# Opening the layers' memory in three steps, with the first projections inside the attention stage, and the attention stage's norm steps moved behind the penalties

## The chip, the cores and the metric

The kernel runs on one core of a Trainium2 chip. A core has five engines that work side by side, each through its own queue in order: TensorE (PE in the profile, with its weight loads as PEld), VectorE (DVE), ScalarE (ACT), GpSimd (POOL) and SyncE (SP), which here issues DMAs. SBUF is the memory that all of them share, PSUM the one that TensorE writes. The metric is device time in microseconds; the median of three runs is given, with the lowest and the highest.

## The reference

Input `x` has 4 batches of 512 tokens of 128 features, all in f32. Two blocks with a residual each:

```python
x = x + attn(layernorm(x))          # 16 heads of 64, 512 x 512 scores, scale 1/8
                                    # penalty -50 above the diagonal, softmax, @ Wr
x = x + layers(layernorm(x))        # 6 layers
```

A layer of the second block is:

```python
x = attn_layer(shift_tokens(x)) + x   # qkv; q, k: l2norm over a head, scales, rotary with xpos;
                                      # softmax over windows of 32 and the window before; @ Wo
x = ffn_layer(shift_tokens(x)) + x    # layernorm * g + b; 128 -> 2 x 341; a * gelu(gate); 341 -> 128
```

`shift_tokens` delays the second half of the features by one token. `layernorm` takes mean and variance over the 128 features.

## The kernel before

Activations are kept transposed, features on the 128 partitions, 512 tokens of a batch along the free axis. The kernel has two stages, and in each the order of the instructions on every engine is the order in which the program writes them (`manual_schedule`). A tile framework adds the waits.

**First stage (lines 132 to 397).** A loop of 64 iterations `m`, each on two blocks of 128 query rows of one pair of heads, plus a 65th that only finishes. Batch `b`, pair of heads `c` and the half `odd` come from `m`: 16 iterations make a batch. An iteration writes, in this order: `times_v1` of work two pairs back, the scores (line 216), the penalties as matmuls on the same banks (229), the first row block's maximum on DVE (241), a v projection (`make_v`, odd iterations, not in the last batch), the transposes of the previous iteration's probabilities (270, copied out by ScalarE at 274 and DVE at 276), the exponentials on ScalarE (247), the next q or k projection (180, 186), the inverse of the sums (256, DVE) and the normalisation on GpSimd (259). A norm's three steps are spread over even iterations and come at the end of each: `mean` (lines 91 to 97: two matmuls with a constant matrix, a subtraction on DVE, a square on ScalarE), `var` (102 to 105: eight small matmuls, then `rsqrt`) and `scale` (110 to 114: four transposes that spread the factor, one product on DVE). `rsqrt` (73 to 85) is a bit trick on DVE and three Newton steps of four instructions each, on the engine that is handed in. `norm_x` of the next batch stands at c = 1, 2, 3 and `norm_x1`, the norm ahead of the second stage, of the batch before at c = 4, 5, 6. `project_out1` (302, 303) closes a batch: 16 matmuls with `wr` and the residual. One PSUM bank, `pj`, serves all projections and norms here; the scores have two pairs of banks, the transposes two banks, `times_v1` one.

**The passage (lines 393 to 400, then 428 on).** After the loop come the last three halves of `times_v1`, then `project_out1` of the last batch. Then the pools of the first stage (`s1`, `ps1`) are closed, and those of the second (`s2`, `ps2`) are opened in the same memory.

**Second stage (from line 400).** 6 layers x 4 batches x 4 blocks of 128 tokens are 96 units. A `slot(n, ...)` handles four units at once, each at another point of its way: unit n+2 (`new`) is projected, rotated and normed; unit n+1 (`nxt`) has its q and k transposed; unit n (`u`) has its scores, softmax and product with v; unit n-1 (`prev`) is projected out. `begin` makes the shifted input (`shift_into`, GpSimd, 416 to 418) and the layer's tables (`layer_tables`, a small DMA at 423 and a product on GpSimd at 425). A unit's way through `new`: `do_project` three times (442), `square` (453, ScalarE), `sum_squares` (458, DVE), `rotate` (463, 467, DVE), `add_rotated` (478, GpSimd), `inverse_norms` (482 and the two seeds on DVE, Newton on GpSimd), `over_norm` (486, GpSimd), `v_windows` (two copies on ScalarE at 520, then 14 to 16 DMAs on SP's queue, 528 to 532). Projections, scores and products with v share three double banks by turns (`two_t`), transposes and the rest two single banks (`one_t`). The first two slots, n = -2 and -1, have no `u`: they fill the pipeline. The last batch's `norm_x1` is called `late`; its three steps stand ahead of slots -2, -1 and 0.

```python
for n in range(-2, len(units) + NT + 3):
    if -2 <= n < 1:
        late[n + 2]()
```

## Time and profile before

| | us |
|---|---|
| median of 3 runs | 2316.82 (2313.41 to 2319.04) |
| the profiled execution, its own time | 2314.14 |
| its span, first to last instruction | 2312.4 |
| start of the first score matmul | 27.17 |
| last transposes of the loop done | 578.7 |
| first scores of the second stage (line 565) | 620.68 |
| scores of the second unit | 638.42 |

The page cuts the span into 40 slices of 57.8 us. Each digit is the busy share of a slice in tenths; the row PEclk is the clock that TensorE was granted.

```
PE   6999999999799999999999999999999999999997
DVE  3665656656678788878877888877888788878773
POOL 1443444444577777766767766767776767766760
PEclk9999999999999999999999999999999999999998
```

The dip in the eleventh slice is the passage between the stages. In the table of instructions in order of time, a row has its start, its duration, engine, line and operation, what it writes and reads, and in brackets how long its engine had been idle and what it waited for. The table of stretches gives for each stretch its length, the busy time of every engine with the number of its instructions, the granted clock, and the share and rate of the DMA engines.

### The profile page before, as it was taken

Reading aid. Unit: us, or ns where it says so; the run is one execution under the profiler, and the core shown is the slowest. Engines: PE = TensorE matmul, PEld = TensorE weight load, DVE = VectorE, ACT = ScalarE, POOL = GpSimd, SP = SyncE. Lnnn points to the kernel's source line nnn. Section 1 sums busy time; section 2 is a strip of 40 time slices with the busy share of each in tenths; the row PEclk is TensorE's granted clock in tenths of the full one; section 3 lists DMA queues with packets and bytes.
Section 4 is the critical chain, followed back from the end, with each engine's and each line's share of the span. In section 5 each row is a group of like instructions: output and inputs, shape, how many; then the busy total and the mean of one; then the engine's idle time right before and its main releaser. Section 6 shows DMA issues by size and latency. Waiting matters only on the chain.

```text
span 2312.4 us, 81596 instructions
## 1 busy us (share of the span) xinstructions
PE 2201.3 (95%) x35088; PEld 1447.7 (63%) x35088; DVE 1710.5 (74%) x2692; ACT 1301.7 (56%) x2166; POOL 1436.1 (62%) x1897
## 2 busy tenths in 40 slices
PE   6999999999799999999999999999999999999997
PEld 3555555555366666666666666666666666666664
DVE  3665656656678788878877888877888788878773
ACT  2554544445255666666666666666566666566662
POOL 1443444444577777766767766767776767766760
PEclk9999999999999999999999999999999999999998
DMA  3000000000222233222322223223332223322220
GB/s 113 1 1 1 1 1 1 1 1 1 46 69 68 63 90 75 62 69 65 90 71 65 71 66 90 68 63 73 73 89 62 71 62 86 80 62 72 66 56 15
DMA packets 91025, 125.81 MB, mean 54 GB/s; under 512 B 25262, under 2 KB 39468, under 8 KB 90668
## 3 DMA queue, kind: packets, MB, share of 16 engines
q1 hardware_dynamic: 90236, 119.02, 21.0%
q8 instruction: 279, 4.57, 0.9%
q10 hardware_dynamic: 432, 1.57, 0.2%
q14 instruction: 78, 0.64, 0.1%
HBM read 20.41 MB, written 1.05 MB: 9 GB/s over the span
## 4 chain that ended last, share of the span: by engine, by line
PE 81%; DVE 14%; ACT 2%; issue 2%; POOL 1%; DMA 1%; SPq 0%; POOLq 0%; ACTq 0%
PE ps_proj L442 19%; PE ps_one L538 13%; PE ps_one L633 7%; PE ps_att L608 6%; PE ps_att L576 6%; PE ps_sc L216 5%; PE ps_o L287 5%; PE ps_pt L270 3%; PE ps_proj L666 3%; PE ps_proj L667 3%; PE ps_proj L680 2%; DVE yt L79 2%; PE ps_sc L229 2%; DVE t L467 2%; DVE rot L463 2%
## 5 line engine op out<-in xcount | busy, mean ns | idle before, releaser
L478 POOL TENSOR_TENSOR rot<-rot,t 128x1024 f32<-128x1024 f32 x192 | 453.9, 2364 | 193.9 <-DVE t L467 188.6
L442 PE MATMUL ps_proj<-wqkv,xs 128*128 128x512 f32 x1152 | 557.5, 607 | 15.3 <-DVE t L467 5.4
L259 POOL TENSOR_TENSOR pr<-pr,den 128x1024 f32<-128x1024 f32 x128 | 240.9, 1893 | 335.3 <-DVE den L256 333.1
L453 ACT ACTIVATE sq<-ps_proj 128x1024 f32<-128x1024 f32 x192 | 196.9, 1025 | 365.9 <-PE ps_proj L442 329.3
L486 POOL TENSOR_TENSOR rot<-rot,ss 128x1024 f32<-128x1024 f32 x192 | 365.4, 1903 | 15.0
L442 PEld LDWEIGHTS ps_proj<-wqkv,xs 128*128 128x128 f32 x1152 | 200.0, 192 | 179.6 <-issue 156.6
L458 DVE TENSOR_REDUCE ss<-sq 128x16 f32<-128x1024 f32 x192 | 233.1, 1214 | 51.4 <-ACT sq L453 50.7
L241 DVE TENSOR_REDUCE nm<-ps_sc 128x2 f32<-128x1024 f32 x128 | 156.0, 1218 | 118.7 <-PE ps_sc L229 118.7
L463 DVE TENSOR_TENSOR rot<-ps_proj,lt 128x1024 f32<-128x1024 f32 x192 | 233.4, 1216 | 0.0
L467 DVE TENSOR_TENSOR t<-ps_proj,lt 128x1024 f32<-128x1024 f32 x192 | 232.8, 1213 | 0.0
L274 ACT COPY pT<-ps_pt 128x512 f32<-128x512 f32 x128 | 75.2, 588 | 264.6 <-PE ps_pt L270 262.9
L633 PEld LDWEIGHTS ps_one<-aT,wo 128*128 128x128 f32 x1536 | 186.3, 192 | 45.3 <-issue 44.5
L538 PE MATMUL ps_one<-ident,rot 128*128 128x128 f32 x1536 | 210.2, 280 | 2.9 <-issue 1.5
L586 DVE TENSOR_REDUCE mx<-ps_att 128x16 f32<-128x1024 f32 x96 | 117.5, 1224 | 97.1 <-PE ps_att L576 95.3
L633 PE MATMUL ps_one<-aT,wo 128*128 128x128 f32 x1536 | 187.3, 275 | 0.4 <-ACT aT L541 0.4
L247 ACT ACTIVATE pr<-ps_sc,nm 128x512 f32<-128x512 f32 x256 | 175.0, 694 | 16.3 <-DVE nm L241 16.3
L82 POOL TENSOR_TENSOR yt<-y 128x32 f32<-128x32 f32 x288 | 68.9, 239 | 181.8 <-DVE y L80 166.6
L538 PEld LDWEIGHTS ps_one<-ident,rot 128*128 128x128 f32 x1536 | 164.4, 141 | 22.1 <-issue 4.6
L608 PEld LDWEIGHTS ps_att<-vw,pT 64*32 64x32 f32 x9216 | 104.0, 106 | 95.5 <-ACT pT L541 54.0
L270 PEld LDWEIGHTS ps_pt<-ident,pr 128*128 128x128 f32 x1024 | 120.0, 142 | 55.9 <-issue 45.8
L608 PE MATMUL ps_att<-vw,pT 64*32 64x65 f32 x9216 | 129.6, 226 | 26.4 <-DVE t L467 15.9
L520 ACT COPY vt<-ps_proj 128x512 f32<-128x512 f32 x192 | 103.1, 589 | 83.2 <-PE ps_proj L442 82.1
(127 smaller groups left out, 4014.8 us busy)
## 6 DMA issues: line engine op xcount, KB each, us to landing
vw<-vt SPq DMA_DIRECT2D x1152, 65.0 KB
vw_first<-vt SPq DMA_DIRECT2D x336, 65.0 KB
wqkv<-in_wqkv_dram SPq DMA_DIRECT2D x18, 512.0 KB
wo<-in_wo_dram SPq DMA_DIRECT2D x6, 512.0 KB
w<-in_w_dram SPq DMA_DIRECT2D x6, 341.0 KB
xr<-in_x_dram SPq DMA_DIRECT2D x4, 256.0 KB
out_dram<-tmp_t SPq DMA_DIRECT2D x4, 256.0 KB
w<-in_w_dram SPq DMA_DIRECT2D x12, 64.0 KB
```

Of the source, the lines that this page charges most:

```text
L259: nc.gpsimd.tensor_tensor(self.pr, self.pr, self.den.unsqueeze(2).to_broadcast([P, 2, S]), ALU.mult)
L270: nc.tensor.transpose(pt[:, k * P : (k + 1) * P], self.pr[:, h, k * P : (k + 1) * P], ident)
L442: mm(p[:, c, :], lhsT=u.xs[:, u.T * P : (u.T + 1) * P], rhs=wpart[j][:, c * 512 : (c + 1) * 512], start=True, stop=True,)
L453: nc.scalar.activation(u.sq, u.p[j], AF.Square)
L458: nc.vector.tensor_reduce(u.ss[:, j * HEADS : (j + 1) * HEADS], heads(u.sq), AX.X, ALU.add)
L463: nc.vector.tensor_tensor(heads(t0), heads(pf), lt[:, u.T, 2 * j].unsqueeze(1).to_broadcast([P, HEADS, HD]), ALU.mult)
L467: nc.vector.tensor_tensor(t1.rearrange("p (h t d) -> p h t d", t=2, d=half), pf.rearrange("p (h t d) -> p h t d", t=2, d=half)[:, :, ::-1, :],
L478: nc.gpsimd.tensor_tensor(u.r[j], u.r[j], u.t1, ALU.add)
L486: nc.gpsimd.tensor_tensor(heads(u.r[j]), heads(u.r[j]), u.ss[:, j * HEADS : (j + 1) * HEADS].unsqueeze(2).to_broadcast([P, HEADS, HD]), AL ...
L538: nc.tensor.transpose(tp[:, c * P : (c + 1) * P], src[:, (4 * g + c) * P : (4 * g + c + 1) * P], ident)
L608: mm(o[j * W : (j + 1) * W, h, c * (HD + 1) : (c + 1) * (HD + 1)], lhsT=u.pT[h * HD : (h + 1) * HD, 4 * g + c, j * W : (j + 1) * W], rhs=u ...
L633: mm(y[:, 0:P], lhsT=wo_w[0][:, c, :], rhs=u.aT[:, c, :], start=(c == 0), stop=(c == NC - 1))
```

## The change

It has four parts.

1. In the first stage's loop the norm steps are written directly behind the penalties (and the v projection), ahead of the previous iteration's transposes, instead of at the end of the iteration. The Newton steps of `norm_x` for all batches but the first, and of every `norm_x1`, go from DVE to GpSimd.
2. The pools are split so that the first stage's memory is given back in three steps: `s1`/`ps1` after the loop, `s1b`/`ps1b` (v, the transposed probabilities, the banks `pj` and `o1`) after the last `times_v1`, `s1c` (`wr`, the last batch's input, the attention outputs) after the last residual. The second stage's tiles are split accordingly into `s2a` and the double banks, `s2b` and the single banks, and `s2`.
3. The first unit's shifted input and tables are made in the loop, in iteration b = 3, c = 2, even. `slot(-2)` becomes `first_slot`, in which the first unit's projections alternate with the last `times_v1`; `project_out1` and its residual go into slot -1, behind the second unit's first projection and its rotation.
4. The three steps of `late` go from slots -2, -1, 0 to slots 1, 2, 3.

```diff
-        return layernorm_steps({}, bank, lambda: x1T[b], out_)
+        return layernorm_steps({}, bank, lambda: x1T[b], out_, eng=nc.gpsimd)
...
-            return layernorm_steps({}, bank1, lambda: x0T[b], out_)
+            return layernorm_steps({}, bank1, lambda: x0T[b], out_, eng=nc.gpsimd if b else nc.vector)
...
             elif odd and b + 1 < B:
                 make_v(b + 1, 0, c - NT)
+            if not odd and 1 <= c <= 3 and b + 1 < B:
+                if c == 1:
+                    norms[b + 1] = norm_x(b + 1)
+                norms[b + 1][c - 1]()
+            if b in range(1, B) and not odd and 4 <= c <= 6:
+                norms1[b - 1][c - 4]()
             if old:
                 old[0].transposes()
...
-            if not odd and 1 <= c <= 3 and b + 1 < B:
-                if c == 1:
-                    norms[b + 1] = norm_x(b + 1)
-                norms[b + 1][c - 1]()
             if b > 0 and c == 1 and odd:
-                project_out1(b - 1)
+                y = bank1()
+                project_out1(b - 1, y)
+                residual1(b - 1, y)
                 norms1[b - 1] = norm_x1(bank1, b - 1)
-            if b in range(1, B) and not odd and 4 <= c <= 6:
-                norms1[b - 1][c - 4]()
-        times_v1(B - 1, NC - 2, 1)
-        for half in range(2):
-            times_v1(B - 1, NC - 1, half)
-        project_out1(B - 1)
+            if b == B - 1 and c == 2 and not odd:
+                start = shifted(0), layer_tables(0)
+        steps[0].close()
...
+    def second_step():
+        nonlocal s2b, ps_one, kT_first, vw_first, vts
+        steps[1].close()
+        s2b = ctx.enter_context(tc.tile_pool(name="s2b", bufs=1))
+        ps_one = ctx.enter_context(tc.tile_pool(name="ps2b", bufs=1, space=PSUM))
...
+    def third_step():
+        nonlocal s2
+        steps[2].close()
+        s2 = ctx.enter_context(tc.tile_pool(name="s2", bufs=1))
...
+    def first_slot():
+        new = units[0]
+        part[0] = 1
+        do_project(new, 0)
+        square(new, 0)
+        times_v1(B - 1, NC - 2, 1)
+        rotate(new, 0)
+        sum_squares(new, 0)
+        add_rotated(new, 0)
+        do_project(new, 1)
+        times_v1(B - 1, NC - 1, 0)
+        square(new, 1)
+        rotate(new, 1)
+        sum_squares(new, 1)
+        add_rotated(new, 1)
+        inverse_norms(new)
+        times_v1(B - 1, NC - 1, 1)
+        second_step()
+        over_norm(new, 0)
+        over_norm(new, 1)
+        do_project(new, 2)
+        v_windows(new, units[1])
...
         if new:
             do_project(new, 0)
             square(new, 0)
+        if n == -1:
+            y = one_t()
+            project_out1(B - 1, y)
...
             rotate(new, 0)
+        if n == -1:
+            residual1(B - 1, y)
+        if new:
             do_project(new, 2)
             v_windows(new, follower(new))
...
             over_norm(new, 1)
+        if n == -1:
+            third_step()
         if nxt:
             carry_k(nxt, follower(nxt))
...
-        for n in range(-2, len(units) + NT + 3):
-            if -2 <= n < 1:
-                late[n + 2]()
+        first_slot()
+        for n in range(-1, len(units) + NT + 3):
+            if 1 <= n < 4:
+                late[n - 1]()
```

`second_step` also holds the memsets of `vts`, `vw_first` and `kT_first`, which stood ahead of the second stage.

More of the change, by code (lines that the diff above doesn't have):

```diff
@@ L85, in rsqrt, with layernorm_steps @@
             eng.tensor_tensor(y if k < 2 else v, y, t, ALU.mult)
-    def layernorm_steps(state, bank, inT, outT, g=None, b=None):
+    def layernorm_steps(state, bank, inT, outT, g=None, b=None, eng=nc.vector):
         def mean():
@@ L104, in var @@
             nc.vector.tensor_scalar(rs, v[:, 0:NT], EPS, None, ALU.add)
-            rsqrt(rs, NT, nc.vector)
+            rsqrt(rs, NT, eng)
         def scale():
@@ L127, in out_, with shift_into, shifted, layer_tables @@
             return xT[b]
-        return layernorm_steps({}, bank, lambda: x1T[b], out_)
-    with tc.tile_pool(name="s1", bufs=1) as s1, tc.tile_pool(
-        name="ps1", bufs=1, space=bass.MemoryType.PSUM
-    ) as ps1, tc.manual_schedule():
+        return layernorm_steps({}, bank, lambda: x1T[b], out_, eng=nc.gpsimd)
+    PSUM = bass.MemoryType.PSUM
+    pre = ctx.enter_context(tc.tile_pool(name="pre", bufs=1))
+    steps = [ExitStack() for _ in range(3)]
+    s1c = steps[2].enter_context(tc.tile_pool(name="s1c", bufs=1, side="right"))
+    s1b = steps[1].enter_context(tc.tile_pool(name="s1b", bufs=1, side="right"))
+    ps1b = steps[1].enter_context(tc.tile_pool(name="ps1b", bufs=1, space=PSUM, side="right"))
+    s1 = steps[0].enter_context(tc.tile_pool(name="s1", bufs=1))
+    ps1 = steps[0].enter_context(tc.tile_pool(name="ps1", bufs=1, space=PSUM))
+    def shift_into(dst, src):
+        nc.gpsimd.memset(dst[HD:P, 0:1], 0.0)
+        nc.gpsimd.tensor_copy(dst[0:HD, :], src[0:HD, :])
+        nc.gpsimd.tensor_copy(dst[HD:P, 1:S], src[HD:P, 0 : S - 1])
+    def shifted(b):
+        xs = pre.tile([P, S], F32, tag="xs", name="xs", bufs=2)
+        shift_into(xs, xT[b])
+        return xs
+    def layer_tables(i):
+        scales = pre.tile([P, 4 * HD], F32, tag="scales", name="scales")
+        nc.sync.dma_start(out=scales, in_=a["scales"][i : i + 1].to_broadcast([P, 4 * HD]))
+        lt = pre.tile([P, NT, 4, HD], F32, tag="lt", name="lt", bufs=2)
+        nc.gpsimd.tensor_tensor(
+            lt.rearrange("p t f d -> p t (f d)"),
+            tabs.rearrange("p t f d -> p t (f d)"),
+            scales.unsqueeze(1).to_broadcast([P, NT, 4 * HD]),
+            ALU.mult,
+        )
+        return lt
+    with tc.manual_schedule():
         wq = s1.tile([P, INNER], F32, tag="wq", name="wq")
@@ L137, in body @@
         wv = s1.tile([P, INNER], F32, tag="wv", name="wv")
-        wr = s1.tile([P, NC, EMB], F32, tag="wr", name="wr")
+        wr = s1c.tile([P, NC, EMB], F32, tag="wr", name="wr")
         pen = s1.tile([P, S], BF16, tag="pen", name="pen")
@@ L153, in bank1 @@
         def bank1():
-            return ps1.tile([P, 512], F32, tag="pj", name="ps_pj", bufs=1)
+            return ps1b.tile([P, 512], F32, tag="pj", name="ps_pj", bufs=1)
         def pt_bank():
@@ L164, in load_x @@
                 nc.tensor.transpose(xp[:, t * P : (t + 1) * P], xr[b][:, t, :], ident)
-            x0T[b] = s1.tile([P, S], F32, tag=f"x0T{b}", name=f"x0T{b}")
+            x0T[b] = (s1 if b + 1 < B else s1c).tile([P, S], F32, tag=f"x0T{b}", name=f"x0T{b}")
             nc.scalar.copy(x0T[b], xp)
@@ L192, in make_v @@
             if t == 0:
-                vs[b, j] = s1.tile([P, NT, 512], F32, tag="v1", name="v1", bufs=3)
+                vs[b, j] = s1b.tile([P, NT, 512], F32, tag="v1", name="v1", bufs=3)
             p = bank1()
@@ L265, in transposes @@
                 if t == 0:
-                    pTs[b, c] = s1.tile([P, 2, NT, S], F32, tag="pT1", name="pT1", bufs=2)
+                    pTs[b, c] = s1b.tile([P, 2, NT, S], F32, tag="pT1", name="pT1", bufs=2)
                 for h in range(2):
@@ L280, in times_v1 @@
             if half == 0:
-                os_[b, c] = ps1.tile([P, S], F32, tag="o1", name="ps_o1", bufs=1)
+                os_[b, c] = ps1b.tile([P, S], F32, tag="o1", name="ps_o1", bufs=1)
             o = os_[b, c]
@@ L295, in times_v1, with project_out1, residual1 @@
             if half == 1:
-                at = aTs[b, c] = s1.tile([P, S], F32, tag="aT1", name="aT1", bufs=NC + 2)
+                at = aTs[b, c] = s1c.tile([P, S], F32, tag="aT1", name="aT1", bufs=NC + 2)
                 nc.vector.tensor_copy(at, o)
-        def project_out1(b):
-            y = bank1()
+        def project_out1(b, y):
             for c in range(NC):
                 mm(y, lhsT=wr[:, c, :], rhs=aTs.pop((b, c)), start=(c == 0), stop=(c == NC - 1))
+        def residual1(b, y):
             nc.vector.tensor_tensor(x1T[b], y, x0T[b], ALU.add)
@@ L357, in body @@
                 now[1].normalise()
-            if not odd and 1 <= c <= 3 and b + 1 < B:
-                if c == 1:
-                    norms[b + 1] = norm_x(b + 1)
-                norms[b + 1][c - 1]()
             if b > 0 and c == 1 and odd:
-                project_out1(b - 1)
+                y = bank1()
+                project_out1(b - 1, y)
+                residual1(b - 1, y)
                 norms1[b - 1] = norm_x1(bank1, b - 1)
-            if b in range(1, B) and not odd and 4 <= c <= 6:
-                norms1[b - 1][c - 4]()
-        times_v1(B - 1, NC - 2, 1)
-        for half in range(2):
-            times_v1(B - 1, NC - 1, half)
-        project_out1(B - 1)
-    s2 = ctx.enter_context(tc.tile_pool(name="s2", bufs=1))
-    ps = ctx.enter_context(tc.tile_pool(name="ps2", bufs=1, space=bass.MemoryType.PSUM))
+            if b == B - 1 and c == 2 and not odd:
+                start = shifted(0), layer_tables(0)
+        steps[0].close()
+    s2a = ctx.enter_context(tc.tile_pool(name="s2a", bufs=1))
+    ps = ctx.enter_context(tc.tile_pool(name="ps2", bufs=1, space=PSUM))
+    s2b = s2 = ps_one = kT_first = vw_first = vts = None
     def load_part(i, j):
@@ L405, in one_t @@
     def one_t():
-        return ps.tile([P, 512], F32, tag="one", name="ps_one", bufs=2)
+        return ps_one.tile([P, 512], F32, tag="one", name="ps_one", bufs=2)
     def heads(ap):
@@ L412, in flat @@
         return pt.rearrange("p a n -> p (a n)")
-    def shift_into(dst, src):
-        nc.gpsimd.memset(dst[HD:P, 0:1], 0.0)
-        nc.gpsimd.tensor_copy(dst[0:HD, :], src[0:HD, :])
-        nc.gpsimd.tensor_copy(dst[HD:P, 1:S], src[HD:P, 0 : S - 1])
-    def layer_tables(i):
-        scales = s2.tile([P, 4 * HD], F32, tag="scales", name="scales")
-        nc.sync.dma_start(out=scales, in_=a["scales"][i : i + 1].to_broadcast([P, 4 * HD]))
-        lt = s2.tile([P, NT, 4, HD], F32, tag="lt", name="lt", bufs=2)
-        nc.gpsimd.tensor_tensor(
-            lt.rearrange("p t f d -> p t (f d)"),
-            tabs.rearrange("p t f d -> p t (f d)"),
-            scales.unsqueeze(1).to_broadcast([P, NT, 4 * HD]),
-            ALU.mult,
-        )
-        return lt
     class Unit:
@@ L451, in square @@
     def square(u, j):
-        u.sq = s2.tile([P, INNER], F32, tag="t1", name="sq", bufs=3)
+        u.sq = s2a.tile([P, INNER], F32, tag="t1", name="sq", bufs=3)
         nc.scalar.activation(u.sq, u.p[j], AF.Square)
@@ L460, in rotate @@
     def rotate(u, j):
-        t0 = u.r[j] = s2.tile([P, INNER], F32, tag="rot", name="rot", bufs=6)
+        t0 = u.r[j] = s2a.tile([P, INNER], F32, tag="rot", name="rot", bufs=6)
         lt, pf, half = u.lt, u.p[j], HD // 2
@@ L465, in rotate @@
         )
-        t1 = u.t1 = s2.tile([P, INNER], F32, tag="t1", name="t1", bufs=3)
+        t1 = u.t1 = s2a.tile([P, INNER], F32, tag="t1", name="t1", bufs=3)
         nc.vector.tensor_tensor(
@@ L491, in over_norm @@
         )
-    kT_first = s2.tile([P, NC, W + P], F32, tag="kT_first", name="kT_first")
-    nc.gpsimd.memset(kT_first[:, :, 0:W], 0.0)
-    vw_first = s2.tile([P, NW, NC, HD + 1], F32, tag="vw_first", name="vw_first")
-    for c in range(2):
-        nc.gpsimd.memset(vw_first[c * HD : c * HD + W, 0], 0.0)
-    vts = [s2.tile([P, 2, NC, HD + 1], F32, tag=f"vt{j}", name=f"vt{j}") for j in range(2)]
-    for t_ in vts:
-        nc.gpsimd.memset(t_[:, :, :, HD : HD + 1], 1.0)
+    def second_step():
[3 more added lines that the diff above has]
+        ps_one = ctx.enter_context(tc.tile_pool(name="ps2b", bufs=1, space=PSUM))
+        vts = [s2b.tile([P, 2, NC, HD + 1], F32, tag=f"vt{j}", name=f"vt{j}") for j in range(2)]
+        for t_ in vts:
+            nc.gpsimd.memset(t_[:, :, :, HD : HD + 1], 1.0)
+        vw_first = s2b.tile([P, NW, NC, HD + 1], F32, tag="vw_first", name="vw_first")
+        for c in range(2):
+            nc.gpsimd.memset(vw_first[c * HD : c * HD + W, 0], 0.0)
+        kT_first = s2b.tile([P, NC, W + P], F32, tag="kT_first", name="kT_first")
+        nc.gpsimd.memset(kT_first[:, :, 0:W], 0.0)
+    def third_step():
+        nonlocal s2
+        steps[2].close()
+        s2 = ctx.enter_context(tc.tile_pool(name="s2", bufs=1))
     def new_kT(u):
@@ L511, in new_vw @@
             return vw_first
-        return s2.tile([P, NW, NC, HD + 1], F32, tag="vw", name="vw", bufs=3)
+        return s2b.tile([P, NW, NC, HD + 1], F32, tag="vw", name="vw", bufs=3)
     def v_windows(u, nxt):
@@ L543, in transpose_q @@
     def transpose_q(u):
-        u.qT = s2.tile([P, NC, P], F32, tag="qT", name="qT", bufs=1)
+        u.qT = s2b.tile([P, NC, P], F32, tag="qT", name="qT", bufs=1)
         for g in range(2):
@@ L718, in begin @@
             return
-        xs = s2.tile([P, S], F32, tag="xs", name="xs", bufs=2)
-        shift_into(xs, xT[u.b])
-        lt = layer_tables(u.i) if u.b == 0 else units[u.n - 1].lt
+        if u.n == 0:
+            xs, lt = start
+        else:
+            xs = shifted(u.b)
+            lt = layer_tables(u.i) if u.b == 0 else units[u.n - 1].lt
         for v in units[u.n : u.n + NT]:
```

## The prediction

> **What bounds the kernel now.** I read the page's engine shares and its chain first, then cut the span into stretches, and only then read single instructions in order of time.

> ```profile
> PE 2201.3 (95%) x35088; PEld 1447.7 (63%) x35088; DVE 1710.5 (74%) x2692; ACT 1301.7 (56%) x2166; POOL 1436.1 (62%) x1897
> ...
> PE 81%; DVE 14%; ACT 2%; issue 2%; POOL 1%; DMA 1%; SPq 0%; POOLq 0%; ACTq 0%
> ```

> TensorE is 95% busy and carries 81% of the chain. No TensorE work is added or removed, so all there is to win is the 5% in which it idles, what it loses to a lower clock, and DVE's 14% of the chain. In both places that the change touches, these lie together. Single iterations of the first stage, and the passage between the stages (stretch, its length, then busy time of PE, PEld, DVE, ACT, POOL, clock, DMA):

> ```profile
> 482.62:489.89 7.27, 7.27 (x49) 4.40 (x47) 3.68 (x5) 3.93 (x10) 1.43 (x1) 1.00 0.01 2
> ...
> 513.22:522.02 8.80, 8.39 (x50) 4.69 (x49) 4.43 (x8) 4.59 (x12) 5.24 (x4) 1.00 0.00 0
> 522.02:528.87 6.85, 6.85 (x49) 4.28 (x47) 4.90 (x7) 4.12 (x11) 1.88 (x2) 1.00 0.01 4
> 528.87:537.59 8.72, 8.31 (x56) 5.36 (x54) 4.75 (x10) 4.42 (x13) 5.58 (x4) 1.00 0.00 0
> 537.59:546.09 8.50, 7.07 (x48) 4.26 (x46) 7.97 (x20) 3.60 (x9) 1.80 (x2) 1.00 0.00 0
> 546.09:554.42 8.33, 7.92 (x52) 4.81 (x51) 4.42 (x8) 4.59 (x13) 5.34 (x4) 1.00 0.01 2
> 578.62:638.42 59.80, 45.16 (x403) 22.68 (x402) 37.93 (x53) 16.75 (x26) 31.85 (x46) 0.91 0.21 48
> ```

> Row 1 is an even iteration without a norm: 7.27, TensorE full. The next five hold the mean (8.80), its plain odd neighbour (6.85), the variance (8.72), the odd iteration behind it (8.50 against 6.85) and the scale (8.33). The last row is the passage: from the first `times_v1` after the loop to the scores of the second unit, 59.8 us with 14.6 us of idle TensorE and a clock of 0.91.

> **Part 1, norm steps in the first stage** (six norms: `norm_x` of three batches, `norm_x1` of three). I lay the even iteration out anew with its own durations, zero at the first score matmul. TensorE ends the penalties at 2.70; DVE's first maximum runs 2.57 to 3.79.

> Mean: TensorE +0.86 (two matmuls of 0.43), DVE's subtraction 3.79 to 4.46, ScalarE's square 4.53 to 5.16. ScalarE is in order, and behind the square now queue the first pT copy (3.34 before, now 5.1), both exponentials and the q copy. The pT copy frees the bank for the second pair of transposes, so TensorE waits 0.5 us there, and 0.1 us for the single `pj` bank: 8.7 against 8.80. The last exponential ends at 9.7, and the next scores' second half may wait 0.25 us for its bank. Sum: 0, between +0.3 and -0.3.

> Scale: TensorE +0.65 and 0.37 waiting for `pj`: 8.25 against 8.33. Gain 0.1.

> Variance: this is where it pays. Now the twelve Newton steps stand on DVE ahead of the next aT copy and maximum:

> ```profile
> 537.08 1.79 DVE L80 TENSOR_SCALAR y<-yt 128x4 int32<-128x4 int32 x1
> ...
> 541.17 0.68 DVE L297 COPY aT<-ps_o 128x512 f32<-128x512 f32 x1
> ...
> 541.77 1.21 DVE L241 TENSOR_REDUCE nm<-ps_sc 128x2 f32<-128x1024 f32 x1
> ...
> 543.64 0.66 PE L270 MATMUL ps_pt<-ident,pr 128*128 128x128 f32 x4 [1.43 <-DVE pT L276]
> ```

> From 536.70 to 541.25 DVE does nothing else, and TensorE then waits 1.43 us for a copy behind it. The odd iteration costs 1.65 us over its neighbour here, 1.81 in the batches with v projections (9.84 against 8.03). With the chain on GpSimd this goes: 1.8. In the even iteration the eight matmuls cost 1.0, the transposes end at 6.3, and `times_v1` closes it at 8.2 against 8.72: 0.5. Together 2.3.

> What hides the chain on GpSimd? The trace has no 4-column Newton step there, but 288 of 32 columns: 0.24 us each, one every 0.32, twelve in 3.8. Starting at 4.6 (rs and the two seeds stay on DVE) it ends at 8.4. The two normalisations queue behind it: instead of starting at 5.84 and 8.1 they run 8.4 to 12.2. Who waits for them is the next iteration's transposes, at 8.2+3.2=11.4 and 8.2+5.2=13.4; the probabilities are there at 10.3 and 12.2. Slack 1.1 and 1.2 us (some 0.2 in the last batch, which projects no v). So the cost is nothing while it holds. [...]

> Sum of part 1: 6 x (0+0.1+2.3) = 14.4; I take 13.8 for bank waits between. Bounds 8 (only the odd iterations heal, some of it taken by the mean) to 18.

> **Part 2, the shift and tables of the first unit go into iteration 52.** GpSimd gains 0.09+0.60+0.61+2.34=3.6 us behind its second normalisation, which ends 2.7 into the next odd iteration; the next one starts at 6.9. It fits. The scales' load moves to the head of SP's queue, past the layer's weight loads: one issue of 0.33 us long before use. Nothing.

> **Part 3, the passage.** Before, nothing of the layers starts until the old pools are empty: GpSimd's first memset waits 15.5 us for `x1T`. Then the last norm, the projections of two units and their rotations share DVE:

> ```profile
> 610.80 1.76 DVE L84 TENSOR_SCALAR yt<-yt 128x4 f32<-128x4 f32 x1
> ...
> 612.59 2.26 DVE L85 TENSOR_TENSOR y<-y,yt 128x4 f32<-128x4 f32 x1
> ...
> 625.85 1.98 PE L442 MATMUL ps_proj<-wqkv,xs 128*128 128x512 f32 x4 [3.39 <-DVE t L467]
> ```

> Single Newton steps swell from 0.17 to 2.26 beside GpSimd's large ones; the late norm holds DVE from 608.86 to 617.23. In the changed order, TensorE in order of time: transposes end 578.7; project q waits for the last pT copy, 579.6 to 581.4; times_v1(6) to 583.3; project k to 585.1; times_v1(7), both halves, to 588.9; project v to 590.7; the second unit's q to 592.4. `project_out1` needs the last aT copy, which stands on DVE behind `inverse_norms`: DVE does aT 583.4, q's rotation and sum to 587.5, k's to 591, then line 482 stalls beside add_rotated until 592.4 (as at 621.79: 1.32 us), seeds to 592.9, aT to 593.7. So TensorE idles 1.5 us, projects out 593.9 to 600.8, then v and k of the second unit to 604.3. GpSimd: Newton 593.1 to 596.9, the memsets of the second step (1.6 us, they too wait for aT), both `over_norm` to 602.4: ahead of the q transposes at 604.3. These and the k transposes share two banks with ScalarE's copies: 607.1. Scores begin at 607.4 and wait 0.65 for the last kT copy, ending 609.7 (before: 620.68 to 622.5). The next projection's bank is free at 609.7; before, TensorE waited 3.39 us there. With the remaining order of that slot (0.9 us for the score bank, as the 1.09 before) the second unit's scores begin at 622.3 instead of 638.42: 16.1 us earlier. SP needs 16 issues of 0.63 for the first unit's v windows, from 598.5 to 608.6, and the second's to 618.7; they are used at 616.7 and some 15 us later.

> Cross-check: of the 14.6 idle and some 4.7 lost to the clock (24 projection matmuls in 7.1 and 7.9 us instead of 24 x 0.43), the walk keeps about 5 and shortens by some 14 to 16.

> Given back: the late norm's steps move into slots 1 to 3, where TensorE is full (58.80 of 61.74 us in 638 to 700): 0.86+1.0+0.65, and 0.4 each for a bank that the o transposes still hold: 3.7. Its Newton adds 3.8 to a GpSimd with some 12 of 15.3 us used; the walk leaves GpSimd 3.6 us less behind than before, which covers it. Net 12.4; bounds 4 (DVE or GpSimd chain sets the first slots) and 16.

> The clock: [...] The trace drops to 0.50 behind a gap of 2.10 us (596.17), but stays at 1.00 behind one of 3.39 (625.85). The longest gap of my walk is 1.5. [...] if a 1.5 us gap drops it as the 2.10 did, about 2 us. I take 0 and keep 2 for the range.

> **Sum.** 13.8+12.4 = 26.2 of the profiled execution's span of 2312.4 gives 2286.2; with the 1.7 us around it 2287.9. The median lies 2.7 above that execution: 2290.6.

> **Rivals.** (a) The passage only moves its wait: u0's norm chain on DVE and GpSimd is as long as TensorE's new work, and a late `over_norm` or aT copy holds transposes and scores. For it: DVE has 19 us of work in a stretch of 28. Against it: `over_norm` has 2 us in hand. Part 3 then brings some 3: 2300. (b) Part 1 brings nothing, since the square in front of ScalarE's copies costs at the mean what the variance gains: 2304. Against it: ScalarE is busy 3.93 of 7.27. (c) Slower: the GpSimd Newton chain holds up the normalisations and so the transposes. It decides from the slack of about 1 us, and outweighs all gains (26.2/6 = 4.4 us a norm) once a step takes over 0.75 us; at 1.0 us a step (0.17 to 2.26 happens on DVE beside GpSimd) each norm loses 7.3: 6 x 7.3 - 26 = 18 us slower, 2335. Against it: 288 steps of the same kind show 0.24 with DVE busy. (d) More than walked: the mean and scale steps lose their waits as well (0.4 us each) and the variance its bank wait: some 6 to 10 us more, 2282.

> **Chances.** As walked 0.63, (a) 0.15, (b) 0.09, (c) 0.06, (d) 0.07. About 0.2% (4.6 us) can be told from no change: faster 0.91, same 0.03, slower 0.06. The range takes (a) and (b)'s better half, and (d): 2280 to 2305.

> **What would show it.** Odd iterations behind a variance at 8.03 or 6.85 instead of 9.84 or 8.50; mean iterations still near 8.8; normalisations late by 2 to 3 us there without a transpose waiting for GpSimd; first scores of the layers near 607, second near 622; a clock of 1.00 throughout the passage; slots 1 to 3 longer by about 1.2 each. It is wrong if transposes wait for GpSimd in norm iterations, or if TensorE idles over 8 us between 579 and 622.

## The result and the profile after

The changed kernel takes 2291.95 us (median of 5, 2288.88 to 2295.78) against 2317.53 before (median of 5): ratio 0.9891, 95% interval 0.9876 to 0.9905. The profiled execution spans 2287.1 us, 25.3 less. The forecast was 2290.6, with a range of 2280 to 2305.

The page of the changed kernel, engine shares and chain:

```profile
PE 2193.9 (96%) x35056; PEld 1445.6 (63%) x35088; DVE 1684.3 (74%) x2608; ACT 1299.6 (57%) x2166; POOL 1453.9 (64%) x1981
...
PE 84%; DVE 11%; issue 2%; ACT 1%; DMA 1%; POOL 0%; SPq 0%; POOLq 0%; ACTq 0%; DVEq 0%
```

DVE has given 84 instructions to GpSimd (the twelve Newton steps of seven norms), and its share of the chain has fallen by 3 points, which TensorE now has. The same stretches as before (length, busy PE, PEld, DVE, ACT, POOL, clock, DMA): five iterations with the last batch's norm (mean, its odd neighbour, variance, its odd neighbour, scale), and the passage up to the second unit's scores:

```profile
499.98:508.31 8.33, 8.17 (x49) 4.70 (x49) 4.58 (x7) 3.85 (x9) 3.59 (x3) 1.00 0.00 0
508.31:515.26 6.95, 6.95 (x49) 4.20 (x47) 4.96 (x8) 4.67 (x14) 3.52 (x3) 1.00 0.01 2
515.26:523.37 8.11, 7.95 (x56) 5.26 (x55) 4.28 (x9) 4.04 (x12) 5.91 (x15) 1.00 0.00 0
523.37:530.22 6.85, 6.85 (x49) 4.28 (x47) 4.96 (x8) 4.07 (x12) 3.67 (x3) 1.00 0.00 0
530.22:538.46 8.24, 7.80 (x51) 4.86 (x51) 4.59 (x8) 4.37 (x13) 5.19 (x3) 1.00 0.01 3
562.73:607.01 44.28, 39.88 (x392) 19.48 (x391) 29.82 (x36) 16.75 (x26) 28.61 (x45) 1.00 0.23 57
```

The odd iteration behind the variance takes 6.85 us, as if there were no norm; it took 8.50. The passage is 15.5 us shorter, 4.4 us of TensorE's idle time is left of 14.6, and its clock is 1.00. What TensorE waited for between the loop's last transposes and the first scores of the layers, before and then after (engine, line and what it waited for; us, times, longest):

```profile
PE ps_proj L442 <- DVE rs L104: 5.0, 1, 5.0
PE ps_proj L442 <- POOL xs L418: 2.1, 1, 2.1
PE ps_one L538 <- ACT qT L541: 0.9, 1, 0.9
PE ps_o L287 <- DVE aT L297: 0.9, 1, 0.9
PE ps_one L93 <- DVE x1T L303: 0.8, 1, 0.8
PE ps_one L110 <- ACT kT_first L541: 0.2, 1, 0.2
```

```profile
PE ps_one L335 <- DVE aT L331: 1.3, 1, 1.3
PE ps_one L567 <- ACT qT L570: 0.9, 1, 0.9
PE ps_proj L459 <- ACT pT L308: 0.8, 1, 0.8
```

The 5.0 and the 2.1 are gone: the projections no longer wait for the shifted input, and not for DVE either, as TensorE has the end of the first stage to do meanwhile.

By place: the loop's last transposes end 15.96 us earlier (562.73 instead of 578.69), the first scores begin 29.6 us earlier (591.08), and the second unit's scores 31.4 us earlier, although the late norm's mean step now stands ahead of them. At the scores of the fifth unit 27.1 us of the lead is left, and 25.3 at the end.

### The profile page after: what moved, and what is told of

Read it like the earlier page. It is cut to its first block, busy times and chain, and to the rows that moved or that the text cites. A ratio compares the mean times of both kernels' runs of the same rounds, so it can differ in the third digit from the quotient of the medians.

```text
span 2287.1 us, 81570 instructions
## 1 busy us (share of the span) xinstructions
PE 2193.9 (96%) x35056; PEld 1445.6 (63%) x35088; DVE 1684.3 (74%) x2608; ACT 1299.6 (57%) x2166; POOL 1453.9 (64%) x1981
## 4 chain that ended last, share of the span: by engine, by line
PE 84%; DVE 11%; issue 2%; ACT 1%; DMA 1%; POOL 0%; SPq 0%; POOLq 0%; ACTq 0%; DVEq 0%
PE ps_proj L459 19%; PE ps_one L567 13%; PE ps_one L662 7%; PE ps_att L637 6%; PE ps_att L605 6%; PE ps_sc L250 5%; PE ps_o L321 5%; PE ps_pt L304 4%; PE ps_proj L695 3%; PE ps_proj L696 3%; PE ps_proj L709 2%; DVE t L484 2%; DVE rot L480 2%; DVE yt L79 2%; PE ps_sc L263 2%
## 5 line engine op out<-in xcount | busy, mean ns | idle before, releaser
L82 POOL TENSOR_TENSOR yt<-y 128x32 f32<-128x32 f32 (+1 forms) x309 | 73.5, 238 | 209.6 <-DVE y L80 193.3
```

## The experiments

All ratios are to the kernel before, timed beside each run on the same chip, with 95% intervals. "Distance" is from the end of the loop's last transposes to the first scores of the layers: 41.99 us before, 28.35 in the changed kernel.

### The loop: which engine, and which place?

**newton_only.** Only the engine of the in-loop Newton steps changes:

```diff
-            rsqrt(rs, NT, nc.vector)
+            rsqrt(rs, NT, eng)      # GpSimd for norm_x of b > 0 and norm_x1 of b < 3
```

> The kernel before, with only the Newton steps of the six in-loop norms on GpSimd; the steps stay at the end of the iteration, the last batch's norm keeps its Newton on DVE. Theory (the gain of the first stage is the Newton chain that stood on DVE ahead of the next aT copy and maximum): the odd iterations behind a variance fall from 9.84 and 8.50 us to about 8.05 and 6.9, the even iterations stay at 8.80, 8.72 and 8.33; loop 6 x 1.75 = 10.5 us shorter, about 2307. Rival (what counts is where the steps stand): those odd iterations hardly change, because the wait is at the end of the iteration, and the time stays within 3 us of the kernel before.

Measured: 0.9955 (0.9941 to 0.997). Odd iterations behind a variance take 8.03 and, in the last batch, 6.84 us; even ones stay at 8.80, 8.73 and 8.33. The theory stands. The last batch's variance and the odd iteration behind it (newton_only, stretches):

```profile
519.03:527.76 8.73, 8.16 (x56) 5.37 (x55) 4.76 (x10) 4.42 (x13) 5.59 (x4) 1.00 0.00 0
527.76:534.60 6.84, 6.84 (x48) 4.28 (x46) 6.08 (x8) 3.75 (x10) 4.33 (x14) 1.00 0.00 0
```

**move_only.** Only the place changes: the two `if` blocks with the steps go ahead of `old[0].transposes()`, as in the change.

> The kernel before, with only the norm steps moved behind the penalties; all Newton steps stay on DVE. Theory (the place alone gives little, as the Newton chain of 2.4 us or more now stands on DVE ahead of a transposed copy and the second maximum): variance iterations grow from 8.72 to about 10.4, the odd ones behind them fall to about 8.0, mean 8.33, scale 8.24; the loop gains 0 to 2 us, 2315 to 2318. Rival (the place gives the gain): variance iterations near 8.1, loop 10 us or more shorter, 2307 or below.

Measured: 0.9974 (0.9963 to 0.9985), the last transposes 7.0 us earlier. The sign was right, the size was not: 0 to 2 us were expected. The variance iteration grows only to 9.58 us, where 10.4 was expected, and the odd one behind it takes 8.03. Why it grows so little shows in DVE's first and last Newton step in the last batch (move_only, instructions in order of time):

```profile
527.02 0.16 DVE L82 TENSOR_TENSOR yt<-y 128x4 f32<-128x4 f32 x1
...
529.21 0.16 DVE L85 TENSOR_TENSOR rs<-y,yt 128x4 f32<-128x4 f32 x1
529.29 0.68 DVE L276 COPY pT<-ps_pt 128x512 f32<-128x512 f32 x1
529.84 0.66 PE L270 MATMUL ps_pt<-ident,pr 128*128 128x128 f32 x4 [1.25 <-ACT pT L274]
```

Here GpSimd is idle, and rs with all its steps takes DVE 2.9 us (526.43 to 529.37), where at the end of the iteration, beside GpSimd's normalisation, it took 4.5. TensorE still waits once, for 1.25 us. The second maximum comes late too (529.89), but no wait of TensorE follows from it: the odd iteration behind takes 6.84 us here, as without a norm. So the pair of variance and odd iteration goes from 18.57 us to 17.6 by the place alone, to 16.76 by the engine alone, and to 16.14 by both.

**norms_only.** Both, with the passage of before.

> The kernel before, with both: the in-loop norm steps behind the penalties and their Newton steps on GpSimd; the passage is that of before. Theory (the two parts of the change are independent): the loop ends 16 us earlier, as in the changed kernel, and all of it reaches the end: about 2301.5. More than newton_only and move_only together, since each takes away the other's obstacle. Rival (part of the gain belongs to the passage, for instance by a DVE that arrives less loaded): 2305 or more.

Measured: 0.9936 (0.9918 to 0.9953), span 2298.3, 14.1 us shorter. The loop's transposes end 15.7 us earlier, and nearly all of it reaches the end. The expectation that both would give more than the two parts together was wrong: the parts make 10.4 and 6.0 us by their ratios, so 16, and both together give 14 to 15.

### What hides the GpSimd chain?

**newton_double.** The changed kernel with six Newton rounds in the in-loop norms.

```diff
-        for k in range(3):
+        for k in range(rounds):     # 6 for the in-loop norms on GpSimd, else 3
```

> The changed kernel, with six Newton rounds instead of three in the six in-loop norms, all on GpSimd (24 instructions of 0.20 us, 0.28 apart, 6.6 us instead of 3.3). Theory (the chain is hidden only while the normalisations behind it reach the next transposes in time; slack about 2 us, under 1 in the last batch): the odd iterations behind a variance grow from 8.03 to about 9.2, in the last batch from 6.85 to about 9.2; 6 to 9 us slower than the changed kernel, 16 to 19 faster than before. Rival (GpSimd has room to spare in the loop): no change against the changed kernel.

Measured: 0.9937 (0.9916 to 0.9958), 10.6 us slower than the changed kernel by the two ratios, with some 6 either way from their intervals; 6 to 9 was expected. The chain is 3.3 us longer; odd iterations behind a variance grow by 1.53 us, in the last batch by 2.70 (6.85 to 9.55), which makes 10.4 over the six norms. The wait is where the theory puts it (newton_double, last batch):

```profile
534.13 0.20 POOL L85 TENSOR_TENSOR rs<-y,yt 128x4 f32<-128x4 f32 x1
534.28 3.74 POOL L293 TENSOR_TENSOR pr<-pr,den 128x1024 f32<-128x1024 f32 x2
536.23 1.09 PE L304 MATMUL ps_pt<-ident,pr 128*128 128x128 f32 x8 [2.38 <-POOL pr L293]
```

3.3 less 1.53 is a slack of 1.8 us, and 0.6 in the last batch. The prediction had 1.1 to 1.2 and 0.2, with a chain 0.5 us too long: nearly the same slack. So the chain is hidden only because it is short: half a chain more would already show.

### What does the mean step cost?

**sq_pool.** The changed kernel with the square of the in-loop norms on GpSimd.

```diff
-            nc.scalar.activation(sq, xc, AF.Square)
+            sq_eng.tensor_tensor(sq, xc, xc, ALU.mult)     # in-loop norms on GpSimd
```

> The changed kernel, with the square of the six in-loop norms as a product on GpSimd instead of an activation on ScalarE. Theory (the square in front of ScalarE's copies and exponentials is what the mean step costs beyond its two matmuls): mean iterations 8.33 to about 8.2, the odd ones behind them 8.14 to 8.03, and iteration 3, with no times_v1 to cover, 9.48 to about 8.0; 2 to 3 us faster than the changed kernel, 27 to 28 faster than before. Rival (the mean's cost is the single bank pj and TensorE's own time): iterations as in the changed kernel, no gain.

Measured: 0.989 (0.9868 to 0.9911), no difference in time to the changed kernel. In the iterations: mean 8.33 to 8.29, the one behind it 8.14 to 8.03 (15.77 to 15.67), iterations 2 and 3 together 16.50 to 15.70; iteration 3 alone is still at 9.24, where 8.0 was expected. That makes 1.5 us, half of what was expected and below what the times can tell. The square on ScalarE does cost, but little. Without it a mean iteration still takes 1.03 us more than a plain one: 0.86 are TensorE's two matmuls, and 0.16 is a gap ahead of the penalties for which no semaphore accounts.

### The passage

**late_only.** The kernel before, with the late norm in slots 1 to 3 and its Newton steps on GpSimd.

```diff
-            if -2 <= n < 1:
-                late[n + 2]()
+            if 1 <= n < 4:
+                late[n - 1]()
```

> The kernel before, with only the last batch's norm moved from slots -2 to 0 to slots 1 to 3 and its Newton steps on GpSimd; pools and order of the passage as before. Theory (the passage is won by filling TensorE with projections while the first stage ends, not by freeing DVE of one norm): scores of the second unit some 4 us earlier than 638.4, given back in slots 1 to 3, so 2317 within 2 us. Rival (the 8.4 us that the late norm holds DVE are the passage's loss): 8 to 12 us faster, 2305 to 2309.

Measured: 1.0002 (0.9994 to 1.0011). The second unit's scores come at 636.65, 1.8 us earlier, where 4 was expected, and slots 1 and 2 take it back. TensorE waits for something else (the two longest waits of late_only, 570 to 690):

```profile
PE ps_proj L442 <- DVE t L467: 6.1, 1, 6.1
PE ps_proj L442 <- POOL xs L418: 4.0, 1, 4.0
```

DVE is rid of the late norm there, but the projections still wait for its rotations, and for the shifted input 4.0 us where it was 2.1. The rival, that the late norm on DVE is the passage's loss, falls.

**seq_tail.** The changed kernel with the order of before in the passage; split pools, early shift and tables and late norm as changed.

```diff
         part[0] = 1
+        times_v1(B - 1, NC - 2, 1)
+        for half in range(2):
+            times_v1(B - 1, NC - 1, half)
+        second_step()
+        y = one_t()
+        project_out1(B - 1, y)
+        residual1(B - 1, y)
+        third_step()
         do_project(new, 0)
...
```

> The changed kernel, with the passage back in its old order: the three last halves of times_v1, the second and third memory step, project_out1 and the residual first, then the first unit's projections; split pools, early shift and tables, and the late norm in slots 1 to 3 stay. Theory (the gain of the passage is that projections and the end of the first stage fill each other's waits): the first unit's first projection starts some 14 us later after the loop's end, DVE and GpSimd then hold transposes and scores, scores of the first unit 34 to 37 us after the last transposes of the loop instead of 28.4; 6 to 8 us slower than the changed kernel, so 17 to 19 us faster than before. Rival (early memory, shift and tables alone bring it): within 2 us of the changed kernel, 25 us faster than before.

Measured: 0.9923 (0.9906 to 0.994), 7.4 us slower than the changed kernel; distance 34.99 us, clock 0.90. The same stretch in the changed kernel and in seq_tail, then the longest waits of TensorE in seq_tail's:

```profile
562.73:591.08 28.35, 25.39 (x81) 10.60 (x81) 16.13 (x19) 7.73 (x12) 15.05 (x22) 1.00 0.14 33
562.32:597.31 34.99, 27.86 (x80) 11.76 (x80) 17.28 (x19) 7.85 (x12) 13.89 (x22) 0.90 0.17 42
```

```profile
PE ps_proj L459 <- DVE t L484: 4.0, 1, 4.0
PE ps_one L567 <- POOL rot L503: 1.5, 2, 0.8
```

So of the 13.6 us that the distance loses, 6.6 are the interleaving. The other 7.0 come with the early memory, the early shift and tables and the late norm's removal together. The last alone brings 0.9 in late_only, no more than the distance varies by itself: before, newton_only, move_only and norms_only, which have the same passage, show 41.1 to 43.3. What early memory and early shift bring each was not taken apart.

**passage_only.** The changed kernel with the norm edits of the loop undone.

> The changed kernel with its first part undone: in-loop norm steps back at the end of the iteration with their Newton steps on DVE; pools, early shift and tables, first slot and late norm as changed. Theory (loop and passage are independent parts): iterations as before, first scores 28.4 us after the last transposes, about 11 us faster than before, ratio near 0.9953, which with norms_only (0.9936) makes the whole (0.9891). Rival (the passage gains only behind the new loop): under 7 or over 15 us.

Measured: 0.9935 (0.9915 to 0.9954), distance 28.35, fifth unit's scores 13.75 us earlier. The ratio makes 15.0 us, where 11 was expected and over 15 would have spoken for the rival; the interval reaches to both sides of that line, and the 13.75 of the trace stays below it. The product with norms_only is 0.9871; with some 0.0026 either way from the two intervals it agrees with the whole, 0.9891: no sign that one part needs the other.

**late_on_dve.** The changed kernel with `late`'s Newton steps on DVE.

> The changed kernel with the late norm's Newton steps, in slot 2, on DVE instead of GpSimd. Theory (DVE is busy some 12 of 16 us there and each step can swell beside GpSimd's large instructions, so that the maximum of the scores comes late): slot 2 longer by 2 to 6 us, 1 to 6 us slower than the changed kernel, 20 to 24 faster than before. Rival (late in slots 1 to 3 is hidden on either engine): within 1 us of the changed kernel.

Measured: 0.9905 (0.9884 to 0.9927), against 0.9878 for the changed kernel on the same chip (after_again); by the medians 6.4 us slower, where 1 to 6 was expected. Slot 2 grew by more than the expected 2 to 6 us, from 15.80 to 23.87. The reason, with GpSimd's rows between DVE's (late_on_dve, in order of time):

```profile
624.81 1.90 POOL L503 TENSOR_TENSOR rot<-rot,ss 128x1024 f32<-128x1024 f32 x1
624.98 1.76 DVE L84 TENSOR_SCALAR yt<-yt 128x4 f32<-128x4 f32 x1
...
626.67 2.34 POOL L495 TENSOR_TENSOR rot<-rot,t 128x1024 f32<-128x1024 f32 x1
626.77 2.27 DVE L85 TENSOR_TENSOR y<-y,yt 128x4 f32<-128x4 f32 x1
...
634.10 3.75 PE L459 MATMUL ps_proj<-wqkv,xs 128*128 128x512 f32 x4 [5.56 <-DVE pr L617]
```

Both steps of four columns end with GpSimd's large instruction, 0.03 us behind it: 624.98+1.76=626.74 and 626.71; 626.77+2.27=629.04 and 629.01. The same lines just before, with no such instruction beside them, took 0.17 us (line 84, 624.14) and 0.16 (line 85, 624.34), so that a step can grow by up to 2.1 us. The maximum of the scores behind the chain starts only at 631.48, TensorE waits 5.56 us for the bank, and its clock is 0.86 over the slot.

### A version with one wait less

**early_aT, sq_pool_early_aT and after_again.** The last wait of over 1 us in the passage is `project_out1` for `aT`, whose copy stands on DVE behind `inverse_norms`:

```diff
-        inverse_norms(new)
         times_v1(B - 1, NC - 1, 1)
+        inverse_norms(new)
         second_step()
```

> sq_pool, and in the first slot the last half of times_v1 with its copy to aT goes ahead of inverse_norms, so that the copy does not stand behind DVE's stalled maximum and the seeds. Theory: project_out1 starts when TensorE is free, the 1.28 us wait for aT goes, the first scores come 1.3 us earlier; 3 to 4.5 us faster than the changed kernel, 28 to 30 faster than before. Rival (the wait only moves to the q transposes, since the norm factors come 0.7 us later): as sq_pool.

> The changed kernel with one line moved: the last half of times_v1 and its copy ahead of inverse_norms in the first slot. Theory: the 1.28 us wait of project_out1 for aT goes and first scores come 26.8 to 27.0 us after the loop's last transposes instead of 28.35; 1 to 2 us faster than the changed kernel on this chip. Rival (sq_pool_early_aT was faster by chance of its execution alone): no difference in the stretch from the last transposes to the first scores.

> The changed kernel itself, on the same chip as these three, to compare with them: 25 us faster than before, ratio 0.9876 to 0.9905.

Measured: sq_pool_early_aT 0.9869 (0.9854 to 0.9885); early_aT 0.9869 (0.9848 to 0.989) beside after_again 0.9878 (0.9859 to 0.9896). In time the step from the changed kernel is not resolved. In the traces it is: the distance is 26.81 us in both kernels with the moved line and 28.35 in the six other executions with the changed order, and the wait for `aT` is not in the list any more. So both have a passage shorter by 1.5 us than the changed kernel; more is not shown.

## Why the prediction was right

**The loop** (13.8 forecast, 15.96 measured). The variance was the step that pays: 8.11 and 8.03 us against forecasts of 8.2 and 8.03, a gain of 2.4 per norm where 2.3 was said. The scale took 8.24 against 8.25. The Newton steps on GpSimd (changed kernel, last batch, first and last, and what queues behind):

```profile
519.61 0.20 POOL L82 TENSOR_TENSOR yt<-y 128x4 f32<-128x4 f32 x1 [1.30 <-DVE y L80]
...
522.71 0.20 POOL L85 TENSOR_TENSOR rs<-y,yt 128x4 f32<-128x4 f32 x1
...
522.86 3.75 POOL L293 TENSOR_TENSOR pr<-pr,den 128x1024 f32<-128x1024 f32 x2
```

The chain takes 3.3 us, 0.20 a step and 0.28 apart. The row of 32 columns (0.32 apart), which the prediction took, was a little dear. late_on_dve shows the alternative on DVE: nine of its twelve steps took 0.16 to 0.31 us, but three swelled to 1.75 to 2.27 beside GpSimd.

The mean was mis-sized. It was forecast to gain nothing, with 8.7 us and then 0.25 for a late bank; measured were 8.33 and 0.11, a gain of 0.36 in each of five norms. The walk let the second transposes wait 0.5 us for the copy behind the square. ScalarE starts that copy about when the walk said (504.99, 5.01 us into the iteration, against 5.1), but TensorE comes to these transposes only at 5.46, straight from the q projection, and does not wait. Rival (b) was right in one place: in iteration 3, where no `times_v1` covers, the scores wait 1.18 us for the exponentials, and it takes 9.48 us against 8.03. sq_pool gets 0.8 us back over iterations 2 and 3. Rival (d) came true in part: the mean gained, the scale did not.

So the 2.2 us above the forecast are four terms of about 0.5 each. The variance brought 14.4 instead of 13.8; the 0.6 taken off for bank waits was not needed; the mean brought 1.8 in five norms and lost 1.3 in the first; and the first two iterations were 0.5 shorter. The last of these is scatter between executions: before had a clock of 0.50 from 44.13 to 47.54 there, and the changed kernel had none.

**The early shift and tables** cost nothing that a trace shows: iterations 52 and 53 take 7.26 and 8.04 us, as before (7.27, 8.03).

**The passage.** From the last transposes to the first scores 28.4 us was forecast and 28.35 measured. That is not a chance of the sum: with the loop's 15.96 taken off, every step of TensorE in the walk up to there is within 0.2 us of the trace, `project_out1` for example at 577.9 and 577.79. Of the three waits left, the walk names the first two, with 0.9 and 1.5 us; they are 0.8 and 1.3. The second unit's scores, with the mean's 1.06 taken off, come 43.2 us after the transposes; forecast 43.6.

**Given back in slots 1 to 3**: 3.7 forecast. In the profiled execution it was 5.4 us (1.06 ahead of slot 1's scores, which are the second unit's, and 4.3 from there to the fifth unit's), in after_again 3.6. The difference is the clock behind one gap in slot 3 (changed kernel, order of time):

```profile
639.04 1.68 PE L605 MATMUL ps_att<-kT,qT 64*32 64x64 f32 x124
...
642.48 0.30 PE L605 MATMUL ps_att<-kT,qT 64*32 64x64 f32 x4 [1.76 <-issue]
642.72 3.30 PE L459 MATMUL ps_proj<-wqkv,xs 128*128 128x512 f32 x4
```

No semaphore accounts for the wait of the last four score matmuls, and the next projection ran for the most part at a clock of 0.50 (from 643.24 on; 3.30 us, where it takes 1.98 in after_again). after_again has a gap of 1.81 us ahead of the same four matmuls, and its clock stays at 1.00. Before had such a gap too in that slot, of 1.10.

The traces do show what goes ahead of these gaps: a transfer on the DMA queue that the page lists as "instruction" (the changed kernel's page; packets, MB, share of the 16 engines):

```profile
q8 instruction: 279, 4.57, 0.9%
```

One landed at 641.21 in the changed kernel, and the gap ends 1.27 us later. In the traces of before and after, 60 to 2150 us, TensorE has three and four gaps of over 1.0 us for which no semaphore accounts. Every one of the seven ends 1.27 to 1.52 us after such a landing, where 3% of all moments lie so. What joins the two, no run here shows.

**The sum** was 26.2, measured 25.3: +2.2 in the loop, +0.4 in the passage, -1.7 in slots 1 to 3, and -1.8 between the fifth unit and the end. That last stretch is 1627.8 us before and 1629.7 after, but 1625.6 in newton_double and 1633.5 in early_aT, which have the changed kernel's code there. So the last term is scatter, and it is why times alone do not resolve steps of 2 us. That the sum came within 1 us of the profiled execution is therefore luck in part: the loop's surplus and the two losses behind it nearly cancel. The mechanism does not rest on that, as the iterations of variance and scale and the passage were met one by one.

Rival (a), a wait that only moves, needed a late `over_norm` or aT copy. In seq_tail `over_norm` holds the transposes for 1.5 us in all; in the changed order it holds nothing, and the aT copy holds TensorE for 1.3 us. Rival (c), normalisations held up by the chain on GpSimd, is real as a mechanism: newton_double reaches it at twice the chain, with a wait of 2.38 us.

## What to carry to other kernels

Lay a stage out anew with its own durations, in order, engine by engine, and look for who is queued behind each moved instruction: here this gave the passage's 28.4 us to within 0.1. Where one stage drains while the next fills, interleave their matmuls by hand and let memory go in steps; to free one engine of work at the same place brought nothing alone (late_only, 1.0002). For a chain of tiny instructions, look at which engine's large instructions run beside it: here it did well on GpSimd, where all 84 steps took 0.19 to 0.20 us. How much time hides such a chain is measured by doubling the chain.

## What the runs showed of the hardware

VectorE's steps of 128x4 with inputs in SBUF that began beside a running GpSimd instruction of 128x1024 ended with it: 1.76 and 2.27 us for 0.17 and 0.16 in late_on_dve. It is no chance meeting: in the trace of before, all 34 such steps that began at least 0.2 us ahead of the end of a GpSimd instruction of 128x1024 ended 0.02 to 0.03 us behind it. The 15 that began there and read a PSUM bank (`rs` from `ps_one`, line 104) took 0.16 us.

```profile
639.83:643.24 3.41, 1.65 (x76) 1.11 (x66) 1.10 (x3) 0.00 (x0) 2.92 (x7) 1.00 0.32 78
643.24:646.65 3.41, 3.41 (x8) 1.85 (x7) 2.04 (x2) 0.53 (x1) 3.33 (x3) 0.50 0.10 25
```

```profile
593.67:597.09 3.42, 1.31 (x3) 0.49 (x3) 0.69 (x1) 0.63 (x1) 2.93 (x8) 1.00 0.24 38
597.09:600.50 3.41, 3.41 (x5) 1.35 (x4) 0.19 (x1) 1.02 (x1) 1.61 (x1) 0.50 0.00 0
```

```profile
620.98:624.40 3.42, 1.48 (x136) 1.30 (x120) 3.32 (x5) 0.00 (x0) 2.71 (x4) 1.00 0.40 97
624.40:627.81 3.41, 1.96 (x4) 0.68 (x4) 3.38 (x5) 0.00 (x0) 2.60 (x11) 1.00 0.36 89
```

The gaps of 1.76 (from 640.73) and 2.10 (from 594.07) lie whole in one stretch, and the clock is 0.50 in the next; that of 3.39 (from 622.46) is cut in two at 624.40, and it stays at 1.00. Yet the 1.28 us (from 576.51) lie whole between 574.97 and 578.38 and did not lower it. And TensorE's busy time in a stretch does not decide alone either: behind 1.48 us there was no fall, behind 1.65 there was. What else counts stays open.
